# Unread and zero-valued products on TensorE at the waits of a two-layer transformer kernel

## The chip, the cores and the metric

One Trainium2 chip, one core. The metric is the device time of one execution in microseconds, the median of the runs. TensorE (PE) multiplies, VectorE (DVE) reduces and does element-wise work, ScalarE (ACT) evaluates functions and copies, GpSimd (POOL) does element-wise work and indirect DMAs, SyncE (SP) issues DMAs.

## The reference

The input has 4 elements of 1024 tokens with 256 channels. Two post-norm layers follow one another:

```
x = layernorm(x + attention0(x))   # 16 heads of 16, q and k normalised per head, rotary positions
x = layernorm(x + ffn0(x))         # gate, up, silu, down, 768 hidden
x = layernorm(x + attention1(x))   # 8 heads of 32, causal, a rank-one term added to the scores
x = layernorm(x + experts(x))      # 16 experts, top 2, 12 of them MLPs 256-1024-256, capacity 512
```

attention1 is what this case calls the second attention. In it, for each element:

```
scores = q @ k.T / sqrt(32), -inf above the diagonal
scores = scores + head_scale * q_proj * k_proj     # folded into q's weights by the kernel
out = softmax(scores) @ v @ w_out
```

The expert layer sends each token's row to the slots of its two experts in order of the tokens, so expert 0 can begin only when the last element's rows have been sent.

## The kernel before

The program is written out in the order in which each engine is to run it (a manual schedule around all but the expert MLPs); an engine runs its own queue in that order and waits there for other engines. Between elements the work is woven: `weave` steps through the units of one attention and puts pieces of other work (projections, feed-forward, routing) between them. `tick()` advances a counter that releases postponed steps (`later`).

The first attention (`Maxima`, `Attend`, lines 467 to 509) alternates with the second. The second attention of an element is `second_units(b)`. It has two groups g of four heads, and its steps are of two kinds:

- `Maxima1.unit` (line 972, tiles mx) computes scores for 128 queries of four heads, one PSUM tile per head, and VectorE takes their row maxima (line 982 with the causal mask, line 986 without). After the last unit of a half, `split` writes the negated maxima as three bf16 parts into nm3 (lines 995 and 997), and `turn(u)` transposes nm3 on TensorE (line 1002, tile ptm) and VectorE copies the result into nmT (line 1005). The very first turn of an element is that of g = 0, u = 0.
- `Attend1.scores` (line 1022, tiles sc) computes transposed scores again, adds the maxima by a product of ones_h with nmT, ScalarE takes the exponential (line 1033), GpSimd masks the diagonal (line 1036). One turn later `Attend1.values` (line 1059) accumulates, for each block of keys kt, the four heads' value sums into one PSUM tile (av, `self.av[0]`) and the sums of the exponentials into another (dn, `self.av[1]`), each head in its own 32 partitions. kt runs from 0 to 4 qb + 3 for query block qb (0 or 1), so a group has 4 and 8 such steps; the last one copies both tiles out and divides (lines 1072 to 1079).

PSUM tiles come from `ps_s`, six banks used in rotation (`tag="s"`), and one bank each in `ps_av` and `ps_m`. The second attention of elements 0 to 2 has the first attention's output projection (line 598, ppa, with turns at 613 and 524) and the feed-forward network of the next element woven in; that of element 3 has the last projections for the attention (line 941, p), routing (transposes 647, router products 722, pl) and VectorE's dispatch steps for elements 2 and 3 by a plan written out by hand.

After the last attention comes the end of the last element: output projection `out3[2]` and `out3[3]` (line 598, ppa), residual and normalisation on VectorE and GpSimd (lines 553 to 568, 110), for each of two blocks a transpose `tu` (line 647, ptxn) and router products `lo` (line 722, pl), then the dispatch of the last 512 tokens: VectorE picks experts (lines 771 to 790), TensorE counts the positions (lines 805 and 806, pos), VectorE makes slots and rows, GpSimd sends them by indirect DMA (line 868), SP loads the rows of expert 0 (line 913, dm) and stores the base of the result (line 884, acc_d). Expert 0 begins with transposes (line 99, ptd), a copy on ScalarE (line 100, dmT) and its first products (line 1506, ph).

`mask_w` is a constant bf16 tile of 128 x 512: zero in its first 384 columns, and in the last 128 zero up to the diagonal and -1e30 above it. `ident_h` is the bf16 identity.

Of the kernel before, what the change touches and what calls it, by code (L numbers as in the profile page):

```python
# [10 lines left out]
F32 = mybir.dt.float32  # L11
# [8 lines left out]
P = 128  # L20
B, S, C = 4, 1024, 256
# [14 lines left out]
def postln_layers_kernel(ctx: ExitStack, tc: tile.TileContext, a: dict, out: bass.AP):  # L36
    nc = tc.nc
# [8 lines left out]
    mask_w = const.tile([P, 512], BF16, name="mask_w")  # L46
# [13 lines left out]
    ident_h = const.tile([P, P], BF16, name="ident_h")  # L60
# [51 lines left out]
    with ExitStack() as main:  # L112
        ps_s = main.enter_context(tc.tile_pool(name="ps_s", bufs=6, space=PSUM))
# [12 lines left out]
        def later(n, fn):  # L126
            due.append((now_at[0] + n, fn))

        def tick():
            now_at[0] += 1  # L130
            run = [f for at, f in due if at <= now_at[0]]
            due[:] = [d for d in due if d[0] > now_at[0]]
            for f in run:
                f()
# [5 lines left out]
        def bank(name, big):  # L140

            if big:
                return ps_s.tile([P, 512], F32, tag="s", name=name)
            return ps_m.tile([P, 512], F32, tag="m", name=name)
# [255 lines left out]
        class Maxima:  # L400
# [52 lines left out]
            def turn(self, s, u, big=False, name=""):  # L453

                pt = bank(f"pt{s}_{self.b}_{self.g}_{u}{name}", big)
                src = tokk if s else self.tok
                for i in range(4):
                    nc.tensor.transpose(  # L458
                        pt[:, i * P : (i + 1) * P], src[:, 4 * u + i].rearrange("p h d -> p (h d)"), ident
                    )  # L460
                nc.scalar.copy((self.kT if s else self.qT)[:, u * 512 : (u + 1) * 512], pt)
# [19 lines left out]
        class Attend:  # L481
# [22 lines left out]
            def values(self, i):  # L504
                qb, kt = i // 8, i % 8
                if kt == 0:
                    self.av = ps_av.tile([P, 512], F32, tag="av", name=f"av0_{self.b}_{self.g}_{qb}")
                for h in range(4):
                    nc.tensor.matmul(  # L509
                        self.av[32 * h : 32 * h + 32, :],  # L510
                        va0[:, kt, 4 * self.g + h, :],
                        self.pes[i, h // 2][:, h % 2, :],
                        start=kt == 0,
                        stop=kt == TB - 1,
                    )
                if kt == TB - 1:
                    self.avs[qb] = act.tile([P, 512], F32, tag="avs", bufs=2, name=f"avs0_{self.b}_{self.g}_{qb}")
                    nc.scalar.copy(self.avs[qb], self.av)
# [85 lines left out]
        def out_project0(b):  # L604

            oTs = {}

            def turn(h, c, big):
                if c == 0:
                    oTs[h] = act.tile([P, 2, 512], F32, tag="hT", bufs=1, name=f"oTa0_{b}_{h}")  # L610
                pt = bank(f"pta0_{b}_{h}_{c}", big)
                for i in range(4):
                    nc.tensor.transpose(
                        pt[:, i * P : (i + 1) * P], oq0[b][:, 4 * h + i, c * P : (c + 1) * P], ident
                    )
                nc.scalar.copy(oTs[h][:, c, :], pt)

            def project(j, big):
                def oT(c, i):
                    t = (2 * j + i) % 4  # L620
                    return oTs[j // 2][:, c, t * P : (t + 1) * P]

                project_out(b, j, oT, w0p, "a0", big)

            out = []
            for h in range(2):
                out += [lambda big, h=h, c=c: turn(h, c, big) for c in range(2)]
                out += [lambda big, j=j: project(j, big) for j in (2 * h, 2 * h + 1)]
            return out
# [21 lines left out]
        def ffn0(b):  # L651
# [28 lines left out]
            def down(j, i, big):  # L680
# [9 lines left out]
                add_residual(b, 2 * j + i, dn[:, :C], "f")  # L690

            out = [lambda big: turn(0, big)]
            for j in range(4):
                out += [whole(gate_up, j, f) for f in range(FF0 // P)]
                if j < 3:
                    out.append(lambda big, j=j: turn(j + 1, big))
                out += [lambda big, j=j, i=i: down(j, i, big) for i in range(2)]
# [224 lines left out]
        def project1(b):  # L922
# [29 lines left out]
                out += [lambda big, j=j, s=s: piece(j, s, big) for s in range(3)]  # L952
            return out

        sc_units = [(qb, kt) for qb in range(2) for kt in range(4 * qb + 4)]

        class Maxima1:
# [39 lines left out]
                        nc.vector.tensor_tensor(m, m, nm3[:, :, :, k], ALU.subtract)  # L997

            def turn(self, u):
                pt = ps_s.tile([P, S], BF16, tag="s", name=f"ptm_{self.b}_{self.g}_{u}")  # L1000
                for i in range(4):
                    nc.tensor.transpose(
                        pt[:, i * P : (i + 1) * P], nm3[:, i].rearrange("p h d -> p (h d)"), ident_h
                    )
                nc.vector.tensor_copy(self.nmT[:, u * 512 : (u + 1) * 512], pt[:, :512])

        class Attend1:
# [40 lines left out]
            def values(self, i):  # L1048
                qb, kt = sc_units[i]
                off = max(0, kt * P - qb * 512)  # L1050
                if kt == 0:
                    self.av = (
                        ps_av.tile([P, 512], F32, tag="av", name=f"av1_{self.b}_{self.g}_{qb}"),
                        ps_m.tile([P, 512], F32, tag="m", name=f"dn1_{self.b}_{self.g}_{qb}"),
                    )
                for k, av in enumerate(self.av):
                    for h in range(4):
                        o = 32 * (4 * self.g + h)
                        nc.tensor.matmul(  # L1059
                            av[32 * h : 32 * h + 32, off:],  # L1060
                            ones[:, :32] if k else va1[self.b][:, kt, o : o + 32],
                            self.pes[i][h // 2][:, h % 2, off:],
                            start=kt == 0,
                            stop=kt == 4 * qb + 3,
                        )
                if kt == 4 * qb + 3:

                    vs, rc = [
                        act.tile([P, 512], F32, tag="avs", bufs=2, name=f"{n}_{self.b}_{self.g}_{qb}")
                        for n in ("avs1", "rc1")  # L1070
                    ]
                    nc.scalar.copy(rc, self.av[1])
                    nc.scalar.copy(vs, self.av[0])

                    def divide(k):
                        q = slice(k * P, (k + 1) * P)
                        nc.vector.reciprocal(rc[:, q], rc[:, q])
                        to = self.oT[:, self.g, qb * 512 + k * P : qb * 512 + (k + 1) * P]
                        nc.gpsimd.tensor_tensor(to, vs[:, q], rc[:, q], ALU.mult)

                    for k in range(4):
                        later(min(1 + k, 3), lambda k=k: divide(k))
# [366 lines left out]

        for _ in range(3):  # L1450
            tick()
        out3[2](True)
        tick()
        out3[3](True)
        tick()
        tu[2](True)
        tick()
        lo[2](True)
        tu[3](True)
        lo[3](True)  # L1460
        assert not due
        steps, rows, ends_, sends, sums = dispatch(3, True, 1)
        for step in sends3[1:] + steps[:5] + rows[:1] + steps[5:] + ends_ + rows[1:] + sends:
            step()

        nc.scalar.activation(spacer2, ones[:, 0:1], AF.Gelu)
        dm0 = tail.tile([P, ECH, ROW], F32, name="dm0")
        load_rows(0, dm0)
# [13 lines left out]
    for e in range(EM):  # L1482
# [19 lines left out]
        for f in range(0, FF1 // P, 2):  # L1502
            ph = ps_big.tile([P, S], F32, tag="big", name=f"ph_{e}_{f}")
            for i in range(2):
                for c in range(2):
# [4 lines left out]
                        start=c == 0,  # L1510
                        stop=c == 1,
# [133 lines left out]
```

## Time and profile before

| | us |
|---|---|
| median of 3 runs | 2412.76 (2399.69 to 2414.96) |
| the profiled execution | 2413.88 |
| its span, first to last instruction | 2412.2 |
| PE busy in the span | 2291.8 (95%) |
| DVE busy | 1381.0 (57%) |
| ACT busy | 1020.0 (42%) |
| POOL busy | 738.2 (31%) |
| mean granted TensorE clock | 0.961 |

The profile is of one execution. Times within it are microseconds from the span's start. A row of the timeline gives the start, the time from the first start to the last end of a group of like instructions, engine, line, operation, output and inputs, tile (partitions x columns of the stationary operand), shape and number; in brackets the idle time ahead of it and what ended it. A matrix product in f32 appears as two records. PEclk is the granted TensorE clock; a stretch's clock is the mean within it. The second attentions begin near 693, 1158, 1610 and 1810 us (elements 0 to 3); the end of the last element runs from 1979 to 2028, the experts from there to 2380.

### The profile page before, as it was taken

To read this page: it belongs to the slowest core of one execution; us is meant where nothing else is said; L and a number is where in the kernel's file an instruction comes from. 1 tells how busy PE (TensorE), PEld (TensorE's weight loads), DVE (VectorE), ACT (ScalarE), POOL (GpSimd) and SP (SyncE) were. 2 spreads that over 40 slices of the span, in tenths; PEclk is the share of its full clock that TensorE was granted. 3 is DMA by queue.
4 is the path that set the end of the run, shared out by engine and by line. 5 is a ranking of instruction groups with operands and counts; after the bars stand their busy time and mean duration, and the time that the engine had idled before them with its cause. 6 is when DMAs were issued, how large, how long until landed. Compare 5 with 4: busy or idle time off the path is not lost.

```text
span 2412.2 us, 36189 instructions
## 1 busy us (share of the span) xinstructions
PE 2291.8 (95%) x14004; PEld 1120.7 (46%) x14004; DVE 1381.0 (57%) x3231; ACT 1020.0 (42%) x2041; POOL 738.2 (31%) x1101
## 2 busy tenths in 40 slices
PE   8999999999999999999999999999999985999994
PEld 5333334444444443344444334445565433666662
DVE  7666667666557476776664877636535774111113
ACT  2665655554533456555334555552332231111112
POOL 5326346152215132553331421211111153222223
PEclk9999999999989999999999999999998786999997
DMA  4143120000000000000100000030000012444434
GB/s 111 51 151 112 60 95 15 1 28 1 1 28 1 1 1 1 33 32 25 48 1 1 1 1 19 32 123 1 1 1 1 1 58 93 98 105 107 107 88 151
DMA packets 78125, 107.78 MB, mean 45 GB/s; under 512 B 8832, under 2 KB 67200, under 8 KB 76288
## 3 DMA queue, kind: packets, MB, share of 16 engines
q1 hardware_dynamic: 48592, 73.34, 9.3%
q0 software_dynamic: 9984, 14.82, 3.2%
q10 hardware_dynamic: 19376, 17.30, 2.4%
q8 instruction: 110, 1.80, 0.3%
q14 instruction: 63, 0.52, 0.1%
HBM read 66.54 MB, written 38.90 MB: 44 GB/s over the span
## 4 chain that ended last, share of the span: by engine, by line
PE 87%; DVE 9%; DMA 1%; issue 1%; ACT 1%; POOL 1%; SPq 0%; DVEq 0%; POOLq 0%; ACTq 0%
PE sc L491 21%; PE av L509 10%; PE ph L1506 7%; PE gu L665 7%; PE py L1522 7%; PE mx L972 5%; PE sc L1022 5%; PE p L941 4%; PE dn L683 3%; PE av L1059 3%; PE ppa L598 3%; PE dn L1059 2%; PE mx L467 2%; DVE masked L982 2%; PE qk L321 2%; PE pt L458 1%
## 5 line engine op out<-in xcount | busy, mean ns | idle before, releaser
L470 DVE TENSOR_REDUCE part<-mx 128x1 f32<-128x512 f32 x1024 | 657.1, 685 | 310.5 <-PE mx L467 304.5
L500 ACT ACTIVATE pe<-sc 128x512 f32<-128x512 f32 x1024 | 554.9, 596 | 414.8 <-PE mx L467 383.8
L467 PE MATMUL mx<-kT,qT 32*128 32x512 f32 x2048 | 604.4, 639 | 0.6 <-DVE part L470 0.3
L491 PE MATMUL sc<-qT,kT 32*128 32x512 f32 x2048 | 586.2, 639 | 0.1
L509 PE MATMUL av<-pe,va 128*32 128x512 f32 x2048 | 272.9, 605 | 0.0
L491 PEld LDWEIGHTS sc<-qT,kT 32*128 32x128 f32 x2048 | 164.9, 183 | 212.1 <-issue 173.7
L1033 ACT ACTIVATE pe<-sc 128x512 f32<-128x512 f32 (+3 forms) x384 | 157.4, 496 | 208.9 <-PE sc L1022 207.4
L982 DVE CUSTOM_DVE_ANT_0 masked<-mx,mask_w 128x128 bf16<-128x128 f32 (+3 forms) x256 | 125.7, 491 | 114.2 <-PE mx L972 85.1
L467 PEld LDWEIGHTS mx<-kT,qT 32*128 32x128 f32 x2048 | 173.6, 183 | 18.8 <-DVE part L470 10.8
L1506 PE MATMUL ph<-dmT,f 128*128 128x512 f32 x384 | 170.2, 601 | 6.9 <-DVE dmT L100 3.5
L1514 ACT ACTIVATE hTm<-ph,b 128x512 f32<-128x512 f32 x96 | 60.8, 684 | 262.0 <-PE ph L1506 262.0
L1522 PE MATMUL py<-f,hTm 128*128 128x256 f32 x768 | 167.7, 379 | 0.0
L1526 POOL DMA_INDIRECT acc_d<-yo,dm x48 | 74.6, 1554 | 286.8 <-DVE yo L1524 246.4
L1522 PEld LDWEIGHTS py<-f,hTm 128*128 128x128 f32 x768 | 145.9, 190 | 25.0 <-issue 5.7
L1523 DVE TENSOR_TENSOR yo<-py,b 128x256 f32<-128x256 f32 x48 | 20.4, 425 | 213.3 <-PE py L1522 213.3
L1036 POOL TENSOR_SCALAR_AFFINE_SELECT pe<-pe 128x256 f32<-128x256 f32 x128 | 51.8, 413 | 294.4 <-ACT pe L1033 292.7
L972 PE MATMUL mx<-kT,qT 32*128 32x512 f32 (+3 forms) x768 | 136.9, 579 | 3.9 <-DVE x L553 3.1
L386 POOL TENSOR_TENSOR ss<-ss,neg_half 128x16 f32<-128x16 f32 x48 | 139.2, 2913 | 0.6
L1022 PE MATMUL sc<-qT,kT 32*128 32x512 f32 (+3 forms) x768 | 129.8, 575 | 4.9 <-ACT w_3a L782 1.5
L509 PEld LDWEIGHTS av<-pe,va 128*32 128x32 f32 x2048 | 40.4, 108 | 192.6 <-issue 188.7
L1506 PEld LDWEIGHTS ph<-dmT,f 128*128 128x128 f32 x384 | 72.8, 192 | 97.4 <-issue 86.7
L665 PE MATMUL gu<-xTf,wg 128*128 128x256 f32 x384 | 107.6, 402 | 3.8 <-DVE hT L678 3.3
(351 smaller groups left out, 2948.6 us busy)
## 6 DMA issues: line engine op xcount, KB each, us to landing
f<-in_fc SPq DMA_DIRECT2D x14, 1024.0 KB, 5.0
f<-in_fc ACTq DMA_DIRECT2D x10, 1024.0 KB, 6.1
disp_d<-empty ACTq DMA_DIRECT2D x12, 520.0 KB, 3.5
xink<-in_xT SPq DMA_DIRECT2D x24, 256.0 KB, 2.8
qk_d<-xs SPq DMA_DIRECT2D x6, 1024.0 KB, 4.5
xr<-qk_d SPq DMA_DIRECT2D x6, 1024.0 KB, 5.3
dm<-disp_d SPq DMA_DIRECT2D x11, 520.0 KB, 3.6
x<-in_x SPq DMA_DIRECT2D x32, 128.0 KB, 2.3
```

Source lines behind the costliest of these rows:

```text
L467: nc.tensor.matmul(sc, self.qT[r, t * P : (t + 1) * P], self.kT[r, u * 512 : (u + 1) * 512], start=True, stop=True)
L470: return lambda: nc.vector.tensor_reduce(self.part[:, t, u, h : h + 1], sc, AX.X, ALU.max, negate=True)
L491: nc.tensor.matmul(sc, self.m.kT[r, kt * P : (kt + 1) * P], self.m.qT[r, qb * 512 : (qb + 1) * 512], start=True, stop=True)
L500: nc.scalar.activation(self.pes[i, h // 2][:, h % 2, :], sc, AF.Exp)
L509: nc.tensor.matmul(self.av[32 * h : 32 * h + 32, :], va0[:, kt, 4 * self.g + h, :], self.pes[i, h // 2][:, h % 2, :], start=kt == 0, stop= ...
L665: nc.tensor.matmul(ps[:, i * 256 : (i + 1) * 256], (wg, wu)[i][:, c, f * P : (f + 1) * P], xT[j][:, c, :], start=c == 0, stop=c == 1,)
L972: nc.tensor.matmul(scs[h][:, :n], qT[r, t * P : (t + 1) * P], kT[r, u * 512 : u * 512 + n], start=True, stop=True,)
L982: nc.vector.tensor_tensor_reduce(masked[:, :n], scs[h][:, :n], mask_w[:, 512 - n :], -1.0, -NEG, ALU.add, ALU.min, part)
L1022: nc.tensor.matmul(scs[h][:, off:], ones_h[r, :] if w else kT[r, kt * P : (kt + 1) * P], (self.m.nmT if w else qT)[r, q], start=w == 0, st ...
L1033: nc.scalar.activation(pe[:, j, off:], scs[2 * hp + j][:, off:], AF.Exp)
L1506: nc.tensor.matmul(ph[:, i * CAP : (i + 1) * CAP], f1[:, c, (f + i) * P : (f + i + 1) * P], dmT[:, c, :], start=c == 0, stop=c == 1,)
L1522: nc.tensor.matmul(py[:, :C], hT[:, f, c * P : (c + 1) * P], f2[:, f, :], start=f == 0, stop=f == FF1 // P - 1)
```

## The change

A helper `warm(n)` takes one PSUM tile from `ps_s` and issues n products of `ident_h` with `mask_w` into it, each overwriting the last; nothing reads the tile. It is called with 12 at the first turn of each element's second attention, ahead of the transposes, and six times in the end of the last element at the places shown in the diff, with 12, 9, 3, 3, 15 and 76. In the last element (b = 3) every step of `values` but the last of a query block also issues three products of a zero tile (the first 128 columns of `mask_w`) with `mask_w` that accumulate zeros into dn. Nothing is removed and no work is moved.

```
+        def warm(n):
+            warmed[0] += 1
+            t = ps_s.tile([P, 512], F32, tag="s", name=f"warm_{warmed[0]}")
+            for _ in range(n):
+                nc.tensor.matmul(t, ident_h, mask_w, start=True, stop=True)
...
             def turn(self, u):
+                if (self.g, u) == (0, 0):
+                    warm(12)
                 pt = ps_s.tile([P, S], BF16, tag="s", name=f"ptm_{self.b}_{self.g}_{u}")
...
+                if self.b == B - 1 and kt < 4 * qb + 3:
+                    for _ in range(3):
+                        nc.tensor.matmul(self.av[1], mask_w[:, :P], mask_w, start=False, stop=False)
                 if kt == 4 * qb + 3:
...
         for _ in range(3):
             tick()
+        warm(12)
         out3[2](True)
         tick()
         out3[3](True)
         tick()
+        warm(9)
         tu[2](True)
         tick()
+        warm(3)
         lo[2](True)
         tu[3](True)
+        warm(3)
         lo[3](True)
+        warm(15)
         assert not due
         steps, rows, ends_, sends, sums = dispatch(3, True, 1)
         for step in sends3[1:] + steps[:5] + rows[:1] + steps[5:] + ends_ + rows[1:] + sends:
             step()
+        warm(76)
         nc.scalar.activation(spacer2, ones[:, 0:1], AF.Gelu)
```

## The prediction

> **What bounds the kernel now.** I read the head of the page, then stretches of one clock window each, then TensorE's timeline around each added product, last the chain of waits. The head of the page:
>
> ```profile
> span 2412.2 us, 36189 instructions
> PE 2291.8 (95%) x14004; PEld 1120.7 (46%) x14004; DVE 1381.0 (57%) x3231; ACT 1020.0 (42%) x2041; POOL 738.2 (31%) x1101
> PEclk9999999999989999999999999999998786999997
> ```
>
> TensorE is busy nearly throughout, so its clock is time. The clock falls below full in the second attentions and above all at the end of the last element. The profiled execution took 2413.88 us, 1.7 beside its span, and the median shown is 2412.76; I sum against 2413.88 and compare with the median.
>
> The clock changes only at multiples of 3.413 us from one another, and is then 1.00 or 0.50. In stretches cut there (columns: PE busy, PEld, DVE, ACT, POOL, clock, DMA):
>
> ```profile
> 1158.80:1162.22 3.42, 3.42 (x25) 2.06 (x20) 2.33 (x13) 1.09 (x2) 0.72 (x1) 1.00 0.44 127
> 1162.22:1165.63 3.41, 3.41 (x15) 1.60 (x14) 2.69 (x11) 1.73 (x3) 0.00 (x0) 1.00 0.36 111
> 1165.63:1169.04 3.41, 1.23 (x6) 0.42 (x4) 2.83 (x9) 0.62 (x1) 0.00 (x0) 1.00 0.73 190
> 1169.04:1172.46 3.42, 2.08 (x17) 1.78 (x18) 2.66 (x14) 0.00 (x0) 0.00 (x0) 0.50 0.79 323
> ...
> 1855.12:1858.54 3.42, 3.31 (x37) 2.23 (x36) 2.77 (x6) 0.79 (x4) 0.29 (x1) 1.00 0.00 0
> 1858.54:1861.95 3.41, 3.41 (x24) 2.31 (x24) 1.20 (x8) 0.59 (x1) 0.48 (x2) 0.50 0.03 5
> ...
> 1875.60:1879.02 3.42, 3.42 (x20) 0.78 (x16) 0.67 (x2) 0.00 (x0) 0.00 (x0) 0.50 0.00 0
> 1879.02:1882.43 3.41, 3.38 (x24) 1.61 (x20) 2.25 (x9) 0.59 (x1) 0.00 (x0) 1.00 0.00 0
> ```
>
> The reader is to see that idleness does not decide: 1855.12 to 1858.54 has 3.31 us busy of 3.42, and half clock follows. So I count **work** instead: each product's columns (an f32 record's 512 columns take 0.44 us, 14.00 us for 32 in the chain), a bf16 record half of that, times the share of the array that its stationary tile covers (32*128 and 128*32 a quarter). From the shapes in the trace, 1855.12 to 1858.54 has 0.44 in av, some 0.35 in dn, 0.27 in sc, 0.1 in the 16-column router products: 1.15 us, 34% of the window. Counted so over all 700 windows, each one that full clock follows has 39% or more of full-rate work (1.33 us), each that half clock follows 38% or less. That rule prices the change; at half clock a window must be 77% dense to rise.
>
> [...]
>
> **The change, part by part.** 226 products, each 512 bf16 columns against a full 128x128 tile. No such row exists. Below: four bf16 products of 512 columns on a quarter of the array each, side by side, move the next instruction by 0.22 us (1200.61 to 1200.83). Above: 0.44, the f32 record, also its price at half clock. I take 0.22, since the f32 product is issued as two records and the bf16 one as one. Following dn, a full-tile transpose starts 0.97 us later (839.56 to 840.53), as a quarter-tile mx does (774.22 to 775.19): no price for the switch. Each warm takes one of six ps_s banks in rotation; the bank six tiles back has been emptied at each place (an ACT copy, exp or a DVE maximum done), and the five tiles behind it look one tile less far back, which costs at most the 0.3 us between two maxima; I take 0.
>
> **First turns.** TensorE waits at the transposes ptm for VectorE's split of the maxima (line 995):
>
> ```profile
> 706.11 0.61 PE L1002 MATMUL ptm<-ident_h,nm 128*128 128x128 bf16 x4 [2.83 <-DVE nm L995]
> ...
> 1170.38 0.61 PE L1002 MATMUL ptm<-ident_h,nm 128*128 128x128 bf16 x4 [3.53 <-DVE nm L995]
> ...
> 1624.01 0.61 PE L1002 MATMUL ptm<-ident_h,nm 128*128 128x128 bf16 x4 [3.24 <-DVE nm L995]
> ...
> 1829.73 0.40 PE L1002 MATMUL ptm<-ident_h,nm 128*128 128x128 bf16 x4 [3.36 <-DVE nm L995]
> ```
>
> Twelve products are 2.64 us and fit the idle time of the last three elements; without that cover they would cost 2.64 each. Queued behind them are ptm, then the copy nmT and the scores; none is late if the clock is full. In the first element the clock has been half since 698.0: 3.6 products at 0.44 lift the window that ends at 704.8 from 0.6 to 1.4 us of work, just enough; the other 8.4 run at 0.22 and end at 706.7, 0.6 late (at half clock throughout it would be 2.4). Then the stretch behind ptm, half speed against full-clock rows of the same instructions (ptm 0.33, mx 1.94, ppa or p 1.92, sc with nmT 1.18, mx of 384 2.23, pta 0.58):
> - element 0: 706.11 to 715.26, 9.15, against 5.37; minus 0.6: gain 3.2
> - element 1: 1170.38 to 1179.50, 9.12, against 5.37: gain 3.75
> - element 2: 1624.01 to 1641.00, 16.99, against 10.1; 0.8 of its mx is waiting for VectorE and stays: gain 6.1
> - element 3: 1830.06 to 1838.89, 8.83, against 5.78: gain 3.05
>
> That is 16.1. A window that starts within 0.9 us of the products' end holds only idle time, ptm and thin mx, and falls anyway: one phase in four, taking back most of a gain, 2 in all. **14**, bounds 6 (two elements fall again) and 16.
>
> **Zero products.** The twenty units of the last element with kt below the last, three each: 60 x 0.22 = 13.2 us, on TensorE, behind dn and ahead of the next mx, whose bank VectorE waits to fill. Half clock there, replaced by the same units at full clock in element 0 with the woven work exchanged: 1860.34 to 1880.24 is 19.9 against 13.64 - 2.50 + 1.59 = 12.7, and 0.75 just ahead: 7.9. 1887.85 to 1907.72 is 19.87 against 11.5; but VectorE has 13.23 us there, and at the 87% that it shows in the next stretch (27.65 of 31.85) it needs 15.2: 4.7. 1944.17 to 1951.72: 7.55 against 4.8: 2.75. 1964.05 to 1971.42: 7.37 against 4.0, of which part turns into the wait for w_3a (1.49 us, ACT behind VectorE): 3.0. Together 18.3. Of the 13.2, some 2.6 vanish in eight turns from 1903 to 1944 that already lose about 1.8 us each to waits (1913.67 to 1921.48 is 7.81 for 6.0 of products; I credit 0.33 a turn), and 1.3 in the wait for w_3a: price 9.3; with no cover 13.2. Three thin stretches (around 1855, 1886 and 1940) stay under 1.31 us' work for half of all window phases even with the fillers; a fall costs about 2.3: 3.4 back. **5.6 net**, bounds -2 (no cover, each thin stretch falls for two windows) and +15 (neither).
>
> **The end.**
>
> ```profile
> 1983.02 5.86 PE L598 MATMUL ppa<-w1o,oT 128*128 128x256 f32 x14 [3.07 <-POOL oT L1079]
> 1991.35 1.23 PE L647 MATMUL ptxn<-ident,x 128*128 128x128 f32 x4 [2.48 <-DVE x L110]
> ...
> 2002.27 0.69 PE L805 MATMUL pos_3b<-oh_3b,before 128*128 128x64 f32 x2 [3.62 <-DVE w_3b L781]
> ...
> 2022.63 1.55 PE L99 MATMUL ptd<-ident,dm 128*128 128x128 f32 x6 [18.96 <-DMA dm<-disp_d]
> 2027.57 1.07 ACT L100 COPY dmT<-ptd 128x512 f32<-128x512 f32 x2 [23.79 <-DMA acc_d<-x]
> ```
>
> No DMA is issued or moved past; the products stand on TensorE's queue alone. 12 products (2.6) lie in 3.07, 9 (2.0) in 2.48, 3 (0.66) in ACT's xTn copy (0.67), 15 (3.3) in 3.62, 76 (16.7) in 18.96; uncovered, the 118 would be 26. At full clock ppa's second half ends 2.1 earlier, so ptxn at 1989.35 (2.0 earlier); the two rounds of ptxn and pl (1.23 and 1.89 against 0.66 and 1.06) bring lg to 1994.1 instead of 1998.75. From there VectorE, POOL's sends, SP's loads and eight stores set the time and all move along: 4.6, and 0.5 in pos. ph then still starts cold: from the end of the 76 to ph lie over 5 us with 0.9 of work. **5.1**, bounds 2 and 7.
>
> Sum: 14 + 5.6 + 5.1 = 24.7; 2413.9 - 24.7 = **2389**, 1.0% under the median.
>
> **Rivals.** *The clock holds everywhere and the fillers hide*: +2 at the first turns, +9 in the sums: 2378. For it: the waits of 1903 to 1944. Against: VectorE at 87%. *The sums do not repay*: VectorE sets the pace or thin stretches fall regardless, and the sums come to -2 (2397); or the clock answers to gaps alone, the zero products bring nothing and cost 9.3 to 13.2 (2404 to 2408). Say 2403. For it: VectorE's 87%; against: 1860 to 1880, where VectorE has 9.45 of 21.70, and the fall at 1858.54 without a gap. [...] *Slower: products with a mostly or wholly zero operand do not count as work.* Then the clock stays as it was, every product is 0.44 where it was half, and the decisive place is the 76: 33 us from 2003.7, to 2037, against ph at 2028.2, with ptd and its copies 3 behind them: +11. Sums +9 to 13, first turns +2 to 3 in two elements at half clock: 2440. It decides if 1991 to 2020 still reads 0.50. Against it: 1158.80 and 1162.22 keep 1.00 only if the transposes pta, whose identity operand is mostly zero, count (40 and 42% with, 28 and 29% without); an all-zero tile is in no row.
>
> **How the numbers follow.** Forecast 0.50 (own range 2381 to 2398), all hidden 0.18, sums do not repay 0.24, slower 0.05, rest 0.03. A measurement tells about 1% (24 us) from no change: the limit is 2388.6, so not quite half of the forecast and all of the first rival are faster, 0.42; the slower rival and the rest give 0.06; 0.52 remain. Range 2376 to 2408: the upper end takes in the second rival, the lower the first. The window phase differs from run to run (runs shown spread 15 us), and either end allows for that.
>
> **What would show it.** Right: clock 1.00 from 1165 to 1180 and 1620 to 1640 and through 1980 to 2010; ppa x14 at 3.5 instead of 5.86; ptm's idle under 1; at most six half-clock windows from the last element's first turn to its last sum; ph at about 2003. Wrong: half clock after ptm in three of four elements; a zero product of 0.3 us or more from start to start; ptd waiting for TensorE instead of the DMA; VectorE over 95% in the last element.

## The result and the profile after

| | before | changed |
|---|---|---|
| median, us | 2406.75 (9 runs, 2399.69 to 2421.98) | 2396.35 (9 runs, 2392.80 to 2398.47) |
| ratio | | 0.9945, 95% interval 0.9919 to 0.9971 |
| profiled execution, us | 2413.88 | 2397.94 |
| its span, us | 2412.2 | 2396.0 |
| half clock in the falls ahead of the experts, us | 157.0 | 54.6 |

The changed kernel is 0.55% faster, some 13 us (7 to 20). It lies in the predicted range, at about half of the predicted gain. The runs also lie closer together: 5.7 us apart against 22.3. Two runs that lie far above the rest of their kernel are left out of the ratios below, one of 2457.11 us of the kernel before and one of 2614.03 of f3_no76. The head of the page after:

```profile
span 2396.0 us, 36641 instructions
PE 2313.0 (97%) x14230; PEld 1123.9 (47%) x14230; DVE 1379.4 (58%) x3231; ACT 1019.5 (43%) x2041; POOL 737.2 (31%) x1101
PEclk9999999999999999999999999998999999999997
```

TensorE is busy 21 us longer and the program ends 16 us earlier. The clock's row says why: only two of its 40 slices are below 9, the one that holds element 2's first turn (the 28th, 1617 to 1677 us) and the last of all, as before. The low slices from the last element's second attention to its end (the 31st to 34th of the profile before) are gone, and so is that at element 0's first turn (the 12th). In stretches cut at this execution's clock windows (columns: PE busy, PEld, DVE, ACT, POOL, clock, DMA), element 1's first turn, element 2's, and two places with little work in the last element:

```profile
1166.11:1169.52 3.41, 2.48 (x14) 1.02 (x13) 2.92 (x13) 0.21 (x1) 0.00 (x0) 1.00 0.82 287
1169.52:1172.93 3.41, 3.41 (x26) 2.68 (x25) 2.69 (x13) 0.00 (x0) 0.00 (x0) 1.00 0.40 153
...
1620.07:1623.49 3.42, 2.06 (x18) 1.33 (x18) 3.07 (x14) 0.00 (x0) 0.73 (x2) 1.00 1.08 436
1623.49:1626.90 3.41, 3.41 (x16) 2.22 (x17) 2.55 (x15) 0.58 (x1) 0.20 (x1) 0.50 0.17 72
1848.77:1852.18 3.41, 3.30 (x29) 2.14 (x28) 2.72 (x5) 0.00 (x0) 0.00 (x0) 1.00 0.00 0
1852.18:1855.59 3.41, 3.41 (x22) 0.88 (x19) 0.47 (x3) 0.78 (x4) 0.77 (x2) 0.50 0.00 0
1855.59:1859.01 3.42, 3.35 (x29) 1.91 (x28) 1.23 (x9) 0.99 (x2) 0.00 (x0) 1.00 0.00 0
```

Element 1 keeps its clock behind ptm, where it had lost it before. Element 2 still falls, at 1623.49. In the last element a fall at 1852.18 lasts one window instead of six. TensorE's timeline, the added products and what follows them (start, length of the group, and in brackets the idle time ahead):

```profile
1165.70 2.75 PE L962 MATMUL warm<-mask_w,ident_h 128*128 128x512 bf16 x12
1169.38 0.40 PE L1013 MATMUL ptm<-ident_h,nm 128*128 128x128 bf16 x4 [0.94 <-DVE nm L1004]
...
1620.66 0.40 PE L1013 MATMUL ptm<-ident_h,nm 128*128 128x128 bf16 x4 [0.65 <-DVE nm L1004]
...
1621.96 0.70 PE L981 MATMUL mx<-kT,qT 32*128 32x128 f32 x4 [0.48 <-DVE x L553]
1622.95 1.86 PE L981 MATMUL mx<-kT,qT 32*128 32x256 f32 x6 [0.29 <-DVE nmT L1016]
...
1841.24 0.82 PE L1080 MATMUL dn<-mask_w 128*128 128x512 bf16 x3
1841.99 1.14 PE L981 MATMUL mx<-kT,qT 32*128 32x512 f32 x8
...
1847.75 0.82 PE L1080 MATMUL dn<-mask_w 128*128 128x512 bf16 x3
1848.41 0.39 PE L1013 MATMUL ptm<-ident_h,nm 128*128 128x128 bf16 x4
...
1971.22 3.62 PE L598 MATMUL ppa<-w1o,oT 128*128 128x256 f32 x16
1977.56 0.87 PE L647 MATMUL ptxn<-ident,x 128*128 128x128 f32 x4 [0.79 <-DVE x L110]
1987.07 16.57 PE L962 MATMUL warm<-mask_w,ident_h 128*128 128x512 bf16 x76
2006.37 0.87 PE L99 MATMUL ptd<-ident,dm 128*128 128x128 f32 x2 [2.73 <-DMA dm<-disp_d]
2012.04 4.37 PE L1527 MATMUL ph<-dmT,f 128*128 128x512 f32 x5 [2.81 <-ACT dmT L100]
```

The waits at ptm, 3.5 and 3.2 us before, are now filled but for 0.94 and 0.65, and ptm still waits for VectorE: the products did not delay it. Products back to back cost 0.22 us each (76 in 16.57); three among the sums cost 0.75 at full clock when an instruction on a quarter tile follows (1841.24 to 1841.99), and mostly 0.66 when one on a full tile does (1847.75 to 1848.41). ppa's sixteen take 3.62 where fourteen took 5.86. ph begins at 2012.04 instead of 2028.21, but its first five records still take 4.37, at half clock.

### The profile page after: what moved, and what is told of

The parts are those of the page before. It is cut to its first block, busy times and chain, and to the rows that moved or that the text cites. A ratio compares the mean times of both kernels' runs of the same rounds, so it can differ in the third digit from the quotient of the medians.

```text
span 2396.0 us, 36641 instructions
## 1 busy us (share of the span) xinstructions
PE 2313.0 (97%) x14230; PEld 1123.9 (47%) x14230; DVE 1379.4 (58%) x3231; ACT 1019.5 (43%) x2041; POOL 737.2 (31%) x1101
## 4 chain that ended last, share of the span: by engine, by line
PE 88%; DVE 8%; issue 1%; ACT 1%; DMA 1%; POOL 1%; SPq 0%; DVEq 0%; POOLq 0%; ACTq 0%
PE sc L491 21%; PE av L509 10%; PE ph L1527 7%; PE gu L665 7%; PE py L1543 7%; PE mx L981 5%; PE sc L1033 4%; PE p L941 4%; PE dn L683 3%; PE av L1070 3%; PE dn L1070 3%; PE mx L467 2%; PE ppa L598 2%; DVE masked L991 2%; PE qk L321 2%; PE pt L458 1%
## 5 line engine op out<-in xcount | busy, mean ns | idle before, releaser
L1033 PE MATMUL sc<-qT,kT 32*128 32x512 f32 (+3 forms) x768 | 121.2, 538 | 3.7 <-DVE part L991 1.3
```

The costliest lines, as they stand in the source:

```text
L1033: nc.tensor.matmul(scs[h][:, off:], ones_h[r, :] if w else kT[r, kt * P : (kt + 1) * P], (self.m.nmT if w else qT)[r, q], start=w == 0, st ...
```

## The experiments

The same landmarks in every profile divide the path. **First turns**: from ptm to the first instruction behind the stretch that was slow (sc at 719.4, ppa at 1181.7, sc at 1641.0 and at 1838.9 in the profile before). **Sums**: from 1838.9 to the last dn (1979.0). **End**: from there to ph. In us, one profile each:

| kernel | el. 0 | el. 1 | el. 2 | el. 3 | sums | end |
|---|---|---|---|---|---|---|
| before | 13.31 | 11.35 | 16.99 | 9.16 | 140.15 | 49.16 |
| changed | 9.53 | 7.61 | 15.34 | 5.92 | 136.18 | 43.62 |
| f0_after | 9.53 | 7.60 | 13.22 | 5.92 | 136.15 | 43.63 |
| g3_after | 9.53 | 7.60 | 15.26 | 5.92 | 136.20 | 43.61 |
| e1_turns | 11.17 | 7.59 | 15.42 | 5.92 | 128.42 | 49.19 |
| e2_sums | 13.03 | 10.95 | 13.41 | 9.25 | 136.11 | 46.97 |
| e3_end | 12.73 | 10.36 | 15.58 | 9.63 | 140.11 | 46.02 |
| e4_quarter | 13.03 | 10.12 | 15.45 | 8.72 | 141.26 | 58.95 |
| f1_turns_end | 11.17 | 7.60 | 13.30 | 5.92 | 135.64 | 46.11 |
| f3_no76 | 9.52 | 7.59 | 13.56 | 5.92 | 140.14 | 46.09 |
| f2_thin | 9.53 | 7.61 | 15.44 | 5.92 | 129.78 | 44.44 |
| g0_thin | 11.17 | 7.60 | 15.39 | 5.92 | 131.43 | 44.43 |
| g2_dense | 9.53 | 7.60 | 15.30 | 5.92 | 133.59 | 43.65 |
| g1_best | 9.52 | 7.60 | 12.35 | 5.92 | 130.11 | 44.40 |

**Each part alone.** The first three leave two of the three parts out, the fourth keeps all with a quarter of the work:

```
e1_turns:   - the zero products in values;  - the six warm() of the end
e2_sums:    - warm(12) in turn;             - the six warm() of the end
e3_end:     - warm(12) in turn;             - the zero products in values
e4_quarter:
-                nc.tensor.matmul(t, ident_h, mask_w, start=True, stop=True)
+                nc.tensor.matmul(t, ident_h[0:32, :], mask_w[0:32, :], start=True, stop=True)
-                        nc.tensor.matmul(self.av[1], mask_w[:, :P], mask_w, start=False, stop=False)
+                        nc.tensor.matmul(self.av[1], mask_w[0:32, :P], mask_w[0:32, :], start=False, stop=False)
```

> Only the 12 products at the four first turns; the sums and the end as before. Theory (the clock of a 3.41 us window follows the work, columns x share of the array, counted in the one before; TensorE's wait at ptm takes the products for nothing): 10 to 14 us faster than before, clock 1.00 behind ptm in three of the four elements, the last element's sums with 40 to 55 us of half clock as before. Rival (the products cost what they bring, the gain lies in the end alone): within 4 us of before.

Measured: 0.9946 (0.9924 to 0.9967), 13.0 us faster (8 to 18). The time came as expected, and in these runs the first turns alone match the whole change. In the profile they gave 10.7 us (50.8 to 40.1), and the clock behind ptm held in two elements rather than three: element 0 lost one window (from 707.1), element 2 three. Half clock in the sums was 17 us, not the 40 to 55 expected: without any product there, this profile's sums took 128.4.

> Only the three zero products in each of 20 steps of the last element. Theory: 15 us of products (0.75 a step in the changed kernel's trace), 18 us of half clock taken back, some of the products in waits for VectorE: 2 to 7 us faster than before. Rival (VectorE sets the pace of that stage, the sums do not repay): 0 to 8 us slower.

Measured: 0.9994 (0.9973 to 1.0015). Neither the gain nor the loss is shown: the interval reaches from 5 us faster to 4 us slower.

> Only the 118 products of the end (12, 9, 3, 3, 15, 76). Theory: ppa's 14 in 3.5 instead of 5.9 us, two rounds of ptxn and pl at full clock, 4 to 6 us faster than before; the first product of expert 0 (ph) still runs at half clock for 3 to 6 us. Rival (the products lie on the chain that ends last, at 12 ahead of ppa and at 3 ahead of pl): within 2 us of before.

Measured: 0.9980 (0.9957 to 1.0002), some 4.8 us faster, with no change just inside the interval; the end took 46.0 instead of 49.2 in the profile.

> All 226 products of the changed kernel, each on 32 rows of the array instead of 128: as long on TensorE, a quarter of the work; the values written are read by nobody or are zeros as before. Theory (work decides): 12 products are 0.66 us of work and a window needs 1.3, so the clock falls at the first turns and in the end as it did before; no gain left there, the sums cost their 13 to 15 us less what hides, the 76 at half clock last 33 us and delay expert 0 by some 10: 10 to 30 us slower than before. Rival (busy time or the absence of gaps decides): as the changed kernel, 10 to 16 us faster than before.

Measured: 1.0052 (1.0031 to 1.0072), 12.5 us slower (7 to 17). The profile shows the cause without any sum, in two windows of the 76, and in the 76 themselves:

```profile
2010.38:2013.80 3.42, 3.42 (x9) 1.17 (x8) 3.21 (x13) 0.00 (x0) 1.93 (x3) 0.50 0.12 41
2013.80:2017.21 3.41, 3.41 (x9) 1.17 (x8) 3.27 (x8) 0.00 (x0) 2.83 (x7) 0.50 0.22 78
```

```profile
1169.39 5.29 PE L962 MATMUL warm<-mask_w,ident_h 32*128 32x512 bf16 x12
1174.62 0.61 PE L1013 MATMUL ptm<-ident_h,nm 128*128 128x128 bf16 x4
...
2007.09 32.60 PE L962 MATMUL warm<-mask_w,ident_h 32*128 32x512 bf16 x76
2039.62 1.97 PE L99 MATMUL ptd<-ident,dm 128*128 128x128 f32 x8
```

TensorE is busy throughout these windows (3.42 of 3.42 us), with no gap, and the clock stays at 0.50 for over 30 us; by the prediction's count they hold 13% of full-rate work. In the changed kernel the same 76 products on the full array ran at 1.00 (1987.07 to 2003.64). The two differ in the share of the array that each product uses, not in busy time or gaps: the rival is out. The 76 now last 32.60 us and expert 0 waits for them (ptd has no idle time ahead of it), which is the mechanism of the slower rival in the prediction, at 58.95 against 49.16.

**Are the zero products worth their place?** The next three kernels ran beside the changed kernel:

> The changed kernel unaltered, as the mark for the three beside it: 10 to 16 us faster than before.

Measured: 0.9955 (0.9938 to 0.9972), median 2395.04.

```
f1_turns_end: - the zero products in values
f2_thin:
-                if self.b == B - 1 and kt < 4 * qb + 3:
+                if self.b == B - 1 and (self.g, i) in ((0, 1), (0, 2), (1, 1), (1, 2), (0, 9), (0, 10), (1, 6)):
f3_no76:      - the zero products in values;  - warm(76)
```

> The changed kernel without its 60 zero products. Theory (they cost their 15 us and take back as much half clock, which depends on the window phase): 13 to 20 us faster than before, within 6 of the changed kernel, its runs further apart than that kernel's. Rival (the zero products repay, 5 us or more): 5 us or more slower than the changed kernel.

Measured: 0.9966 (0.9946 to 0.9986), median 2399.33; 4.3 us behind the changed kernel by medians, 2.6 by ratios, and the intervals overlap. It is 8 us faster than before (3 to 13), less than the 13 to 20 expected. The spread came as expected: four of its twelve runs lie from 2388.1 to 2390.0, eight from 2398.8 to 2404.2, and none between; the changed kernel's twelve lie from 2390.8 to 2399.5. In the table, the sums without products are anything from 128.4 to 140.2 (five profiles, mean 136.9), with all twenty steps 136.1 to 136.2 in four profiles.

These times go with the window phase, that is, how far into a 3.413 us window of the clock the sums begin. Without zero products they begin 0.84 to 0.89 us into one in the three profiles in which they take 140.1 or 140.2, with 51 us of half clock; 1.99 us in f1_turns_end, with 135.6 and 38 of half clock; 2.25 us in e1_turns, with 128.4 and 17. The four profiles with all twenty steps begin within 0.54 to 0.75 us, so that they agree does not show that the products make the sums independent of the phase. At near phases the twenty bring 4 us in the sums (136.2 against 140.1); over all five profiles without products they bring 0.7. The end adds to that: it takes 43.6 us with zero products at all twenty steps and 46.0 to 46.1 without them (e3_end, f1_turns_end, f3_no76), 2.5 us more. In the runs, the zero products buy evenness and little mean.

> The changed kernel with zero products at 7 of the 20 steps, those in and next to stretches of little work (kt 1 and 2 of the first query block in both groups, kt 5 and 6 of the second in group 0, kt 2 in group 1). Theory: 13 x 0.75 = 9.8 us of products less, of which a quarter was hidden, and most falls of the clock still prevented: 4 to 8 us faster than the changed kernel. Rival (each step without products falls again): as the changed kernel or slower.

Measured: 0.9933 (0.9906 to 0.9960), median 2389.51, 5.5 us ahead of the changed kernel by medians, as expected; its six runs end at 2390.71, where the twelve of the changed kernel begin at 2390.82. The sums took 129.8.

> Without the zero products and without the 76 at the very end. Theory (expert 0 begins with half clock either way, since between the 76 and its first product lie 5 us with little work): within 2 us of the kernel with the 76, and ph begins equally late behind pos. Rival (the 76 keep the clock for expert 0): 2 to 3 us slower than with them, since ph's first 32 take 16.2 instead of 14.0 us.

Measured: 0.9968 (0.9946 to 0.9990). By ratios it is 0.5 us from f1_turns_end, by medians 2, too close to tell the two expectations apart by time alone. The profiles tell: the end takes 46.09 us against 46.11, so the 76 bring nothing. In TensorE's timeline with the 76 (first two lines) and without (last two):

```profile
2008.36 0.69 PE L99 MATMUL ptd<-ident,dm 128*128 128x128 f32 x2 [2.53 <-DMA dm<-disp_d]
...
2014.04 8.25 PE L1523 MATMUL ph<-dmT,f 128*128 128x512 f32 x14 [3.36 <-ACT dmT L100]
```

```profile
2010.62 1.69 PE L99 MATMUL ptd<-ident,dm 128*128 128x128 f32 x6 [18.96 <-DMA dm<-disp_d]
...
2016.26 8.28 PE L1522 MATMUL ph<-dmT,f 128*128 128x512 f32 x14 [2.99 <-ACT dmT L100]
```

The idle time ahead of ptd, 18.96 us, is back, and ph's first fourteen records take 8.28 us against 8.25.

**Place, element 2, and the best version.**

```
g0_thin:  f2_thin once more
g1_best:  f2_thin,  - warm(76), and in Maxima1.unit behind its four products:
+                if (self.b, self.g, t) == (2, 1, 0):
+                    warm(5)
g2_dense: the changed kernel with zero products at the 13 steps that f2_thin leaves out
```

> The kernel with zero products at 7 of 20 steps once more, beside the changed kernel: 4 to 8 us faster than it if place decides; within 2 if its 2389.5 was a matter of window phase.

Measured: 0.9924 (0.9895 to 0.9952), median 2391.92, 4.6 us ahead of the changed kernel beside it, in the range expected if place decides. It can as well be the smaller number of products (g2_dense below). The sums took 131.4, beginning 0.52 us into a window, and 129.8 in f2_thin, beginning 2.27 us into one. At that second phase the seven steps gain nothing: e1_turns, at 2.25, took 128.4 without any product.

> The changed kernel unaltered, as the mark beside the other three: 10 to 14 us faster than before.

Measured: 0.9947 (0.9927 to 0.9968), median 2396.50.

> Zero products only at the other 13 of the 20 steps, first turns and end as in the changed kernel. Theory (they cost 9.8 us where no window was short of work): the thin stretches fall as without products, 3 to 9 us slower than the changed kernel. Rival (any product counts alike wherever it stands): between the changed kernel and the one with 7 steps.

Measured: 0.9941 (0.9920 to 0.9961), median 2394.82. A miss: I expected it 3 to 9 us behind the changed kernel, and it is level with it. Both halves of the twenty steps alone do better in the profile's sums (129.8 and 131.4 for the seven, 133.6 for the thirteen) than all together (136.2). The sums with the thirteen begin 0.59 us into a window, so with g0_thin (0.52) and the four profiles with all twenty (0.54 to 0.75) this compares like phases. So the twenty are too many. Half clock in the sums is 14 us with all twenty, 14 to 17 with the seven, and 20 with the thirteen, which speaks for the places of the seven, but the intervals of the times do not show it.

> The 7 steps, no 76 at the end, and 5 more products in element 2 between the two units of maxima behind ptm, where TensorE waits for VectorE and the trace shows a fall in every run with the 12 products alone. Theory (a window with under 1.3 us of work falls; the 5 are 1.1 us of work, some 0.8 of it in waits): element 2's stretch from ptm in 11 instead of 13.2 to 15.4 us, 2 to 4 us faster than the kernel with the 7 steps, the missing 76 worth nothing. Rival (the stretch waits for VectorE, not for the clock): as the kernel with the 7 steps or 1 us slower.

Measured: 0.9920 (0.9891 to 0.9948), median 2389.93; its six runs end at 2392.02, where the twelve of the changed kernel beside it begin at 2392.52. It is faster than the kernel before and the changed kernel; against the seven steps alone its 2.0 us by medians are within the noise. Element 2 is shown by the profile, TensorE's timeline and then the windows:

```profile
1621.45 0.48 PE L981 MATMUL mx<-kT,qT 32*128 32x128 f32 x2 [0.48 <-DVE x L553]
1621.87 1.25 PE L962 MATMUL warm<-mask_w,ident_h 128*128 128x512 bf16 x5
1623.05 1.18 PE L981 MATMUL mx<-kT,qT 32*128 32x256 f32 x8
```

```profile
1620.36:1623.77 3.41, 2.93 (x24) 1.59 (x22) 2.84 (x14) 0.00 (x0) 0.93 (x2) 1.00 0.95 393
1623.77:1627.19 3.42, 3.42 (x23) 1.70 (x21) 2.54 (x12) 0.90 (x2) 0.00 (x0) 1.00 0.03 14
```

The clock holds, and the stretch takes 12.35 us, not the 11 expected, but less than in any of the other thirteen profiles (13.2 to 17.0).

## Why the prediction was right or wrong

**The count of work** held in this case's profiles, and it is what carried the prediction. Made anew over all fourteen (9784 windows of 3.413 us, from 8 us after the start, each product's work spread evenly over its record), every window with 39% or more of full-rate work was followed by full clock and every one with 36% or less by half clock. Between the two lie 58 windows of either kind, so the count is good to a few hundredths. The prediction's "all 700 windows" is too wide by the first two of the profile, which hold 0 and 25% and are followed by full clock. The all-zero tile, which no row before showed, counted like any other: the windows of the changed kernel that start at 1852.18, 1882.90 and 1934.10 hold 44, 50 and 48% with the zero products, 26, 32 and 29% without, and full clock followed each. Gaps did not decide: e4_quarter, busy for 3.42 of 3.42 us, stayed at 0.50.

**The first turns** were put at 14. From profile to profile they gave 50.8 - 38.4 = 12.4; against the mean of the four kernels without those products or with a quarter of their work (48.3) the nine kernels with only the 12 products have a mean of 38.3, so 10.0. Elements 0, 1 and 3 came within 1 us of their terms. The term that failed is element 2, put at 6.1: it gave 1.65 in the profile, and 0.7 between the means (15.4 without, 14.7 with). There the products for the maxima behind ptm wait for VectorE's residual (x, line 553) and for nmT, so the window from 1620.07 has 2.06 us of busy time and 0.65 us of work, and the clock falls at 1623.49, though the window ahead of it (1616.66 to 1620.07) was busy for 3.36 of 3.41 us. I had allowed for that in one phase of four; the trace before showed the wait (0.8 us in mx), and I took it as time that stays, not as work that lacks. Five more products in that wait kept the clock (g1_best), which shows the cause.

**The zero products** were put at 5.6 net: 14.9 us regained from half clock (18.3 less 3.4) for a price of 9.3. The profiles of the change give 140.15 - 136.18 = 4.0; against the mean without products it is 0.7, and e2_sums finds nothing. Two terms were wrong. The price: in the changed profile the twenty groups move the next instruction by 16.0 us in all, against 13.2, and TensorE's idle time in the sums falls from 6.1 to 3.0, so 3.1 were covered, against 3.9. The net price was 12.9 instead of 9.3. I had found no charge for changing from full to quarter tiles, and 0.1 a group is there; two groups fell into half clock and cost 1.25 and 1.39. The 2.3 a fall, from which the 3.4 comes, was an estimate of mine that no run shows; the single windows of half clock told of below cost 1.4 to 1.6. And what half clock costs there: in this pair of profiles 16.9 came back (4.0 and 12.9), even more than I had put, but that is one phase, with 51 us of half clock in the stretch, where f1_turns_end without products had 38 and e1_turns 17.

**The end** was put at 5.1 and gave 5.5 in the profile (49.16 to 43.62), 3.1 with the products of the end alone: up to 2.5 of it need the zero products ahead (43.6 against 46.0 to 46.1 us). ppa, ptxn and pl moved much as worked out, and that ph starts at half clock all the same, so that the 76 bring nothing, was shown by f3_no76 and by the kernels with the seven steps (44.40 without the 76, 44.44 and 44.43 with them).

**The base.** I summed against the profiled execution, 2413.88, as if it were typical; nine runs put the median at 2406.75, 7 us lower. That the forecast of 2389 lies only 7 us below the measured 2396, with a gain of 24.7 forecast and 13 measured, is luck of that base: from 2406.75 the same gain would have given 2382. A profile with long falls flatters whatever prevents falls. The difference shows on the other side too: outside these stretches the changed kernel's profile lost 5.8 us, 1.4 to 1.6 in each of the four stretches up to a first turn, each with a window of half clock that the profile before does not have (at 196.7, 749.7, 1186.6 and 1644.0). The sum did not contain these. 12.4 + 4.0 + 5.5 - 5.8 is the 16.1 by which the spans differ. By the means the same sum is 10.0 + 0.7 + 3 to 5.5, 14 to 16, and 13 was measured.

**The rivals.** The measured 2396 is also what the first half of the second rival gives (2397, the sums at -2), and by the means the sums, at 0.7, lie nearer to it than to 5.6. Its mechanism is not what the profile shows: VectorE was busy 96 of the 136 us of the sums, and half clock there fell from 51 to 14 us. The other half of it, a clock that answers to gaps alone, is refuted by e4_quarter (no gap, 0.50 through 32.60 us of products), and the slower rival by the windows with the all-zero tile (44 to 50%, full clock behind them) and by the 76 products at 1.00.

## What to carry to other kernels

Read the clock by the windows that the trace shows, and count work beside busy time: in these runs a window with 39% or more of full-rate work was followed by full clock, one with 36% or less by half clock, and zeros served as well as data. Fillers paid here in waits that ended later than they did (0.94 and 0.65 us of idle time were left at ptm); among the real products twenty groups cost 16.0 us and bought mostly evenness, and seven did better (2389.5 against 2395.0 us beside them). Count it anew in another kernel's trace before relying on it. Before pricing a gain from one profile, ask whether that execution was typical for what the change prevents, price it from several, and compare stretches that begin at the same window phase.

## What the runs showed of the hardware

TensorE, busy without a gap, stayed at half clock for over 30 us while each product used a quarter of the array (e4_quarter: 76 products on 32 rows in 32.60 us at 0.50; on 128 rows in the changed kernel 16.57 us at 1.00). A stationary tile of zeros counted in full (changed kernel: 44, 50 and 48% in three windows that would hold 26, 32 and 29% without it, and full clock behind each). From full to quarter tiles the next instruction started 0.31 us behind the third product instead of 0.22 (0.75 us from the first of three, 1841.24 to 1841.99, against 0.66, 1847.75 to 1848.41). And the program without zero products in its last element falls into two groups of runs some 10 us apart (f1_turns_end: 2388.1 to 2390.0 and 2398.8 to 2404.2; f3_no76: 2389.8 to 2391.5 and 2399.8 to 2403.4). In five profiles of such programs the sums take 128.4 to 140.2 us, and which of these goes with where they begin within a clock window. That this makes the two groups is likely but not shown, since no run of either faster group was profiled.
